# Router of a sparse feed-forward layer: logits of two token tiles in each strip of 32 rows, and one transpose for the logits and for the mask

## The chip, the cores and the metric

The kernel runs on one core of a Trainium2 chip. The time is the device time of one execution in microseconds; the kernel before was measured three times (1661.81, 1661.89 and 1663.59 us, median 1661.89). The engines are named as in the profile: PE is TensorE, PEld its weight loads, DVE VectorE, ACT ScalarE, POOL GpSimd, SP the queue that issues most DMA transfers.

## The reference

All is in float32, for 8 sequences of 512 tokens with 256 channels. Four layers follow one another, each as `x = x + layer(layernorm(x))`: an attention with 16 heads in which only the 307 queries of the highest score spread per head keep a result; an expert layer; a gated linear attention over the sequences as time steps, followed by a gated feed-forward; and the same expert layer once more. The change is in the expert layer:

```python
prob = softmax(xf @ router_w.T + router_b)            # 4096 tokens x 16 blocks
_, idx = top_k(prob, 4)
mask = zeros((n, 16), bool).at[arange(n)[:, None], idx].set(True)
h = einsum('nd,ibd->nib', xf, w1b) + b1b              # 16 blocks of 64 hidden units
h = relu(where(mask[:, :, None], h, 0))
y = einsum('nib,dib->nd', h, w2b) + b2
```

So for each token a router gives 16 logits, the four most probable blocks are kept, and the 64 hidden units of every other block are set to zero. The kernel computes all 1024 hidden units and multiplies them with the mask.

## The kernel before

The residual `xres` stays in SBUF: 128 tokens as partitions, then sequence b (8 of them), slice k (the token's place in its sequence divided by 128, 4 of them) and 256 channels. The attention comes first and takes up to about 585 us; what follows works on one slice k at a time, which is 8 tiles of 128 tokens, one of each sequence, in two groups g of four tiles.

Work on a slice comes as two kinds of Python generators. The "units" are the heavy matmuls: `out_projection` (L780), `routed_ffn` (the hidden layer h_ps at L911, then `down` with y_ps at L891), and `swiglu` (L938). The "pieces" prepare a later slice: `route` (the router) and `gla` (the gated linear attention). `between(units, pieces, n)` issues a unit and then as many pieces, up to the next `yield`, as spread n of them evenly over the units. This sets the program's order roughly; the build then moves neighbouring instructions of an engine by its own costs. Each engine runs its instructions in order. There are eight routers: `route(k, (1, k))` for the first expert layer, `route(k, (2, k))` for the second; ten pieces each.

A router goes like this. The slice's tokens are normalized by ACT (L742), and `to_channels` turns them by PE transposes (L752) into xT[g]: 128 channels as partitions, two halves c, 512 tokens (four tiles of 128). Four matmuls (L810) take the weights `rw[:, c, :]` (128 channels x 32, of which 16 columns are the router's and 16 are zero) as the stationary side and 512 tokens as the moving side; each writes its own strip of 32 PSUM partitions, so the two halves c of a group are in two strips and are not yet summed. ACT copies the 128x512 result to `lgT` (L814). Four matmuls (L820) then turn it: `lgT` in blocks of 128 tokens is the stationary side, and `sel`, 128x32 with ones where two strips' rows belong to one logit, is the moving side; this sums the halves and gives tokens as partitions, with 32 columns (two tiles' 16 logits) for each block. DVE and ACT then compute the softmax (L826 to L839), the top four of each tile (L844, L848: chosen places become 4.0) and the 0/1 mask (L853, 128 tokens x 8 tiles x 16 blocks). Eight PE transposes (L859) turn the mask of each tile into 16 rows of 128 tokens, ACT casts it to bytes (L860, one cast for each group), and two transfers (L864) store it to DRAM as `md[g, j, f, token]`, where block 2f + j covers half j of hidden chunk f. Four transfers (L869) load it back, each row block spread over 64 partitions, as `mk`. In the expert layer ACT (or DVE) makes h from h_ps (L919, L917), and DVE multiplies it with `mk` (L920); then y_ps uses it.

All DMA transfers here are issued by SP, in order. The `post` pool has two buffers for each tag (`lgT` and `mT` have one). At the start of this part SP issues the loads of the weights one after another: rb, rw (L602), w1, b1, w2, b2, q_w and so on; POOL clears `rw` and makes `sel` (L634 to L638); DVE finishes the attention (L628) and uses part of q_w (L681).

## Time and profile before

| what | value |
|---|---|
| median of three runs | 1661.89 us |
| the profiled execution | 1659.83 us |
| its span, first to last instruction | 1658.1 us |
| granted TensorE clock | 0.991 |
| PE busy, of the span | 1605.9 us, 97% |
| DVE busy | 968.2 us, 58% |
| ACT busy | 680.1 us, 41% |
| POOL busy | 334.8 us, 20% |

The profile is of one execution. The busy time of PE counts every pass of a matmul from its start to its modelled end, so passes overlap in it. "The chain that ended last" is found by going back from the last instruction, at each step to what released it or to the instruction before it on its engine; its shares say which engine set the end. In a timeline or a chain a piece is given with its start in us from the span's start, its length and its work. A weight load row (PEld) belongs to the matmul pass behind it. A form such as "128*32 128x512" names the part of the array (rows*columns) and the moving tile.

### The profile page before, as it was taken

The numbers are of one execution on the slowest core, as the hardware profiler recorded it, in microseconds if no ns is written. First come the engines' busy times: TensorE is split into PE (matmuls) and PEld (weight loads), VectorE is DVE, ScalarE is ACT, GpSimd is POOL, SyncE is SP. The second block draws the span as 40 slices with busy tenths as digits, with TensorE's granted clock in tenths as the row PEclk, the third lists the DMA queues.
The fourth block names the chain that finished last, engine by engine and source line by source line (L and its number), as shares of the span: only waits on it lengthen the run. The fifth ranks groups of instructions, "written<-read, shape, count | busy, mean of one in ns | idle before, by whom it ended". The sixth has DMA issues, their size and how long they took to land.

```text
span 1658.1 us, 19533 instructions
## 1 busy us (share of the span) xinstructions
PE 1605.9 (97%) x7298; PEld 823.9 (50%) x7298; DVE 968.2 (58%) x2007; ACT 680.1 (41%) x1216; POOL 334.8 (20%) x384
## 2 busy tenths in 40 slices
PE   7999999999999969999989999999999999999999
PEld 3423323333233247655564556555655655766666
DVE  6977777676666785437663566267265533344242
ACT  2366666666656814352346123622521452121110
POOL 3011111010100112114342342144233320000000
PEclk9999999999999979999999999999999999999999
DMA  3100000000000051010000001000000010011100
GB/s 108 40 2 3 3 2 3 2 3 2 2 3 3 2 164 26 6 34 13 1 1 0 1 1 27 0 0 0 1 1 1 0 26 0 20 33 37 41 26 26
DMA packets 23234, 27.55 MB, mean 17 GB/s; under 512 B 4932, under 2 KB 19684, under 8 KB 23140
## 3 DMA queue, kind: packets, MB, share of 16 engines
q1 hardware_dynamic: 22068, 24.74, 5.1%
q10 hardware_dynamic: 1072, 1.57, 0.3%
q8 instruction: 57, 0.93, 0.2%
q14 instruction: 37, 0.30, 0.1%
HBM read 21.19 MB, written 4.33 MB: 15 GB/s over the span
## 4 chain that ended last, share of the span: by engine, by line
PE 77%; DVE 14%; ACT 3%; POOL 3%; issue 2%; DMA 1%; SPq 0%; ACTq 0%; POOLq 0%; DVEq 0%
PE y_ps L891 16%; PE h_ps L911 11%; PE s L433 8%; PE s L422 8%; PE swi_ps L938 7%; PE proj_ps L1021 7%; PE av L442 7%; DVE pr L1054 2%; DVE pr L1044 2%; PE ao_ps L780 2%; DVE mx L425 2%; PE gla_y L1146 2%; PE q_ps L316 2%; PE v_ps L376 2%; PE k_ps L316 2%
## 5 line engine op out<-in xcount | busy, mean ns | idle before, releaser
L425 DVE TENSOR_REDUCE mx<-s 128x1 f32<-128x512 f32 x512 | 329.0, 684 | 129.0 <-PE s L433 83.0
L437 ACT ACTIVATE e<-s 128x512 f32<-128x512 f32 x512 | 276.1, 599 | 179.1 <-PE s L433 103.5
L422 PE MATMUL s<-k,q 32*128 32x512 f32 x1024 | 298.9, 638 | 2.5 <-ACT k L367 1.8
L433 PE MATMUL s<-q,k 32*128 32x512 f32 x1024 | 294.3, 638 | 0.4 <-DVE mx L425 0.3
L891 PE MATMUL y_ps<-w,h 128*128 128x256 f32 x1024 | 232.2, 382 | 3.5 <-DVE h L920 3.5
L911 PE MATMUL h_ps<-xnT,w 128*128 128x512 f32 x512 | 230.3, 598 | 4.1 <-ACT h L919 4.1
L891 PEld LDWEIGHTS y_ps<-w,h 128*128 128x128 f32 x1024 | 194.1, 192 | 40.9 <-issue 11.1
L911 PEld LDWEIGHTS h_ps<-xnT,w 128*128 128x128 f32 x512 | 95.5, 191 | 114.8 <-issue 106.1
L920 DVE TENSOR_TENSOR h<-h,mk 128x512 f32<-128x512 f32 x128 | 97.8, 777 | 82.2 <-ACT h L919 58.3
L442 PE MATMUL av<-e,va 128*32 128x512 f32 (+1 forms) x1120 | 141.9, 568 | 3.8 <-ACT e L437 2.4
L919 ACT ACTIVATE h<-h_ps,b 128x512 f32<-128x512 f32 x96 | 65.5, 684 | 176.9 <-PE h_ps L911 176.8
L422 PEld LDWEIGHTS s<-k,q 32*128 32x128 f32 x1024 | 89.6, 183 | 84.9 <-DVE mx L425 56.5
L896 DVE TENSOR_TENSOR xres<-xres,y_ps 128x512 f32<-128x512 f32 x48 | 32.8, 684 | 163.6 <-PE y_ps L891 149.3
L433 PEld LDWEIGHTS s<-q,k 32*128 32x128 f32 x1024 | 88.1, 183 | 80.8 <-ACT e L437 53.8
L938 PE MATMUL swi_ps<-zT,w_gate 128*128 128x512 f32 x256 | 122.0, 596 | 4.7 <-DVE h L947 4.6
L938 PE MATMUL swi_ps<-zT,w_up 128*128 128x512 f32 x256 | 121.2, 594 | 0.0
L891 PE MATMUL y_ps<-w_down,h 128*128 128x256 f32 x512 | 116.6, 380 | 0.0
L1021 PE MATMUL proj_ps<-q_w,rT 128*128 128x512 f32 x256 | 116.5, 594 | 0.0
L891 PEld LDWEIGHTS y_ps<-w_down,h 128*128 128x128 f32 x512 | 95.8, 190 | 21.1 <-issue 9.5
L944 ACT ACTIVATE h<-swi_ps 128x512 f32<-128x512 f32 x64 | 38.2, 596 | 157.4 <-PE swi_ps L938 157.3
L1071 POOL TENSOR_TENSOR o<-o,pr 128x512 f32<-128x512 f32 (+2 forms) x56 | 81.1, 1449 | 58.9 <-DVE pr L1054 56.9
L802 POOL TENSOR_TENSOR xres<-xres,b 128x512 f32<-128x512 f32 x32 | 40.0, 1268 | 245.5 <-ACT row L742 223.1
(193 smaller groups left out, 1734.6 us busy)
## 6 DMA issues: line engine op xcount, KB each, us to landing
mk<-md SPq DMA_DIRECT2D x32, 256.0 KB
xres<-in_L_attn_a_x SPq DMA_DIRECT2D x8, 512.0 KB
out<-xres SPq DMA_DIRECT2D x16, 256.0 KB
q<-negT SPq DMA_DIRECT2D x128, 2.0 KB
neg<-negT SPq DMA_DIRECT2D x128, 2.0 KB
w<-in_f_w1T SPq DMA_DIRECT2D x1, 1024.0 KB
w<-in_f_w2T SPq DMA_DIRECT2D x1, 1024.0 KB
w_gate<-in_b_w_gateT SPq DMA_DIRECT2D x1, 1024.0 KB
```

Of the source, the lines that this page charges most:

```text
L316: nc.tensor.matmul(ps, w[:, c, bass.ts(m, P)], xnT[:, c, :], start=(c == 0), stop=(c == NC2 - 1),)
L422: nc.tensor.matmul(s, qs[e][rows, m, bass.ts(k, P)], ks[e][rows, m, :], start=True, stop=True)
L425: nc.vector.tensor_reduce(mx[:, b, 2 * e + m, r : r + 1], s, AX.X, ALU.max)
L433: nc.tensor.matmul(s, ks[e][rows, m, bass.ts(kt, P)], qs[e][rows, m, :], start=True, stop=True)
L437: nc.scalar.activation(ex, s, AF.Exp, scale=1.0 / DH**0.5)
L442: nc.tensor.matmul(av[32 * j : 32 * j + 32, queries], va[:, 8 * kt + 4 * m + j, e, :], es[j][:, queries], start=(kt == 0), stop=(kt == 3 a ...
L891: nc.tensor.matmul(y[0][:, bass.ts(i, D)], h[f][:, bass.ts(2 * u + i, P)], w[:, f, :], start=(f == 0), stop=(f == NF - 1),)
L911: nc.tensor.matmul(ps, w1[:, c, bass.ts(f, P)], xT[g][:, c, :], start=(c == 0), stop=(c == NC2 - 1),)
L920: nc.vector.tensor_tensor(hf, hf, mk[g][:, f, :], ALU.mult)
L938: nc.tensor.matmul(ps, w[:, c, bass.ts(f, P)], zT[g][:, c, :], start=(c == 0), stop=(c == NC2 - 1),)
L1021: nc.tensor.matmul(ps, rT[b // G4][:, c, bass.ts(b % G4, P)], q_w[:, c, m], start=(c == 0), stop=(c == NC2 - 1),)
L1071: nc.gpsimd.tensor_tensor(dst, dst, src, ALU.add)
```

## The change

The logits are summed over the channel halves in PSUM. `rw` gets two versions h of the weights, one with the 16 router columns at places 0 to 15 and one at 16 to 31, zeros elsewhere; the weights are loaded by two transfers. Sixteen matmuls of 128 tokens each go through the four versions (h, c) and, for each, through four tiles: tile b = 2s + h goes to strip s, where all four versions are accumulated into the same 32 rows. So the strips hold the logits of two tiles each, 128x128 in all. `lgT` is 128x128, and one transpose turns it; `sel` is no longer there. The mask is written by two DVE instructions, one for each group, into a tile `taken` whose free axis has the order of `md` (g, j, f, tile). One transpose turns it to 128 rows of 128 tokens, one cast makes bytes of it, and one transfer stores it.

```diff
-        rw = wpool.tile([P, NC2, 32], F32, name="rw")
+        rw = wpool.tile([P, NC2, 2, 32], F32, name="rw")
         nc.gpsimd.memset(rw, 0.0)
-        nc.sync.dma_start(
-            out=rw[:, :, 0:NBLK], in_=t["f_router_wT"].rearrange("(c p) e -> p c e", p=P)
-        )
+        for h in range(2):
+            nc.sync.dma_start(
+                out=rw[:, :, h, bass.ts(h, NBLK)],
+                in_=t["f_router_wT"].rearrange("(c p) e -> p c e", p=P),
+            )
...
-    sel = wpool.tile([P, 2 * NBLK], F32, name="sel")
-    nc.gpsimd.memset(sel, 0.0)
-    for g in range(2):
-        rows = bass.ts(g, 64)
-        nc.gpsimd.tensor_copy(sel[rows, bass.ts(g, NBLK)], i32[rows, 0:NBLK])
...
-        ps = bank_l("lg_ps")
-        for c in range(NC2):
-            for g in range(2):
-                r = 32 * (2 * g + c)
+        ps = bank_l("lg_ps")[:, 0:P]
+        for n in range(2 * NC2):
+            h, c = divmod(n, NC2)
+            for b in range(h, NB, 2):
                 nc.tensor.matmul(
-                    ps[r : r + 32, :], rw[:, c, :], xT[g][:, c, :], start=True, stop=True
-                )
-        lgT = post.tile([P, 512], F32, tag="lgT", name="lgT", bufs=1)
+                    ps[bass.ts(b // 2, 32), :], rw[:, c, h, :],
+                    xT[b // G4][:, c, bass.ts(b % G4, P)],
+                    start=(n == 0), stop=(n == 2 * NC2 - 1),
+                )
+        lgT = post.tile([P, P], F32, tag="lgT", name="lgT", bufs=1)
         nc.scalar.copy(lgT, ps)
         yield
-        ps = bank_l("lg_ps2")[:, 0 : NB * NBLK]
-        for i in range(G4):
-            nc.tensor.matmul(
-                ps[:, bass.ts(i, 2 * NBLK)], lgT[:, bass.ts(i, P)], sel, start=True, stop=True
-            )
+        ps = bank_l("lg_ps2")[:, 0:P]
+        nc.tensor.transpose(ps, lgT, ident)
...
-        nc.vector.tensor_scalar(pr, prob[:, :, 0:NBLK], 2.0, None, ALU.is_ge)
+        taken = post.tile([P, 2, 2, NF, G4], F32, tag="pr", name="taken")
+        for g in range(2):
+            nc.vector.tensor_scalar(
+                taken[:, g],
+                prob[:, bass.ts(g, G4), 0:NBLK].rearrange("p i (f j) -> p j f i", j=2),
+                2.0, None, ALU.is_ge,
+            )
         yield
-        mT = post.tile([NBLK, 2, 512], U8, tag="mT", name="mT", bufs=1)
-        for g in range(2):
-            ps = bank_l("mT_ps")
-            for i in range(G4):
-                nc.tensor.transpose(ps[0:NBLK, bass.ts(i, P)], pr[:, 2 * i + g, :], ident)
-            nc.scalar.copy(mT[:, g, :], ps[0:NBLK, :])
+        ps = bank_l("mT_ps")[:, 0:P]
+        nc.tensor.transpose(ps, taken.rearrange("p g j f i -> p (g j f i)"), ident)
+        mT = post.tile([P, P], U8, tag="mT", name="mT", bufs=1)
+        nc.scalar.copy(mT, ps)
...
-        for j in range(2):
-            nc.sync.dma_start(out=md[:, j].rearrange("g f l -> f g l"), in_=mT[j::2])
+        nc.sync.dma_start(out=md.rearrange("g j f (i t) -> (g j f i) t", t=P), in_=mT)
```

## The prediction

> **What bounds the kernel now.** I read the page first (share of each engine, then the chain that ended last), then that chain cut to single stages, then the rows of the tiles that the change touches.

> ```profile
> span 1658.1 us, 19533 instructions
> PE 1605.9 (97%) x7298; PEld 823.9 (50%) x7298; DVE 968.2 (58%) x2007; ACT 680.1 (41%) x1216; POOL 334.8 (20%) x384
> PE 77%; DVE 14%; ACT 3%; POOL 3%; issue 2%; DMA 1%; SPq 0%; ACTq 0%; POOLq 0%; DVEq 0%
> ```

> TensorE (PE) is busy for 97% of the span and carries 77% of the chain. A busy PE need not be a useful one, so I ask what it does at the router. Here is the chain between 1420 and 1545 us, where the routers of slices 2 and 3 run beside an expert layer; the columns are start, duration and work, and "x8" counts passes.

> ```profile
> 1423.47 0.87 PE mT_ps L859 x8
> ...
> 1441.97 0.44 PE chT_ps L752 x4
> ...
> 1453.64 6.87 PE h_ps L911 x16
> 1460.51 0.99 PE lg_ps L810 x8
> 1461.51 5.35 PE h_ps L911 x12
> 1466.86 0.81 PE lg_ps L820 x8
> 1467.67 1.80 PE h_ps L911 x4
> 1469.46 13.81 PE y_ps L891 x64
> 1483.28 0.87 PE mT_ps L859 x8
> ```

> There is nothing but PE in this stretch: each piece begins where the last one ended, so a microsecond of router work is a microsecond of the kernel. The stage sums say where else that holds (length, then busy us and instructions of PE, PEld, DVE, ACT, POOL):

> ```profile
> 605.00:760.00 155.00, 154.93 (x627) 103.21 (x628) 76.54 (x268) 62.57 (x107) 23.80 (x28) 0.99 0.12 38
> 980.00:1060.00 80.00, 78.97 (x333) 51.61 (x333) 38.53 (x112) 37.95 (x65) 21.25 (x23) 1.00 0.06 14
> 1320.00:1658.00 338.00, 334.15 (x1244) 216.83 (x1242) 121.21 (x300) 74.37 (x123) 19.95 (x16) 1.00 0.09 26
> ```

> All eight routers lie in these three stages. The stages between them, where DVE, ACT and POOL lead the chain, hold none; they start from a PE result and so begin earlier by what PE gained before.

> **The change part by part.** The rows of the tiles (duration min/median/max in ns):

> ```profile
> L810 PEld LDWEIGHTS lg_ps<-xnT,rw x64: 106/108/109, 629.6 to 1520.3; 128*32 128x32 f32 x64
> L810 PE MATMUL lg_ps<-xnT,rw x64: 592/605/617, 629.6 to 1520.7; 128*32 128x512 f32 x64
> L820 PE MATMUL lg_ps<-sel,lgT x64: 192/276/276, 632.4 to 1527.2; 128*128 128x32 f32 x64
> L859 PE MATMUL mT_ps<-ident,pr x64: 272/272/273, 641.1 to 1543.7; 128*16 128x128 f32 x64
> L860 ACT CAST mT<-mT_ps x16: 557/570/575, 641.7 to 1544.1; 16x512 uint8<-16x512 f32 x16
> ```

> There are 64 passes in 8 routers at each line, so 8 a router: an f32 matmul is two passes (4 matmuls at L810 and at L820), a transpose is one (8 at L859; L752's "0.44 x4" is 0.109 us for each transpose).

> *Turning the logits (L820).* Four matmuls, 8 passes: 0.81 us in the chain, and the four h_ps passes behind them take 1.80 instead of 4 x 0.429 = 1.72, since their weights still queue. Together 0.89. One 128x128 transpose, at L752's 0.109, replaces them: 0.78 saved.

> *Turning the mask (L859).* Eight transposes, 0.87, become one, 0.11: 0.76 saved.

> *The logits (L810).* Four matmuls over 512 columns become sixteen over 128, i.e. 8 passes become 32. Each of the four strips of 32 output rows gets 8 passes of 128 columns where it had 2 of 512; the columns streamed are the same. Now 0.99 us in the chain (from the first pass's start to the last one's last column 0.90: two times 0.429 and a stagger of some 7 ns a strip; the rest is the array emptying), and 0.20 more behind it (12 h_ps passes take 5.35, not 5.15). A pass of 128 columns costs 0.109 in L859's and L752's rows, so 8 x 0.109 and the same stagger make 0.89: no change, if the weights of the next pass load under the running one and the strips stay side by side. The trace has no strip pass of 128 columns. The nearest row is gh_ps (L985), same form, two strips with four passes each:

> ```profile
> 725.44 0.14 PEld L985 LDWEIGHTS gh_ps<-rT,q_wg 128*32 128x32 f32 x4 [0.33 <-issue]
> 725.90 0.12 PEld L985 LDWEIGHTS gh_ps<-rT,q_wg 128*32 128x32 f32 x2 [0.31 <-issue]
> 726.33 0.12 PEld L985 LDWEIGHTS gh_ps<-rT,q_wg 128*32 128x32 f32 x2 [0.31 <-issue]
> 725.44 1.91 PE L985 MATMUL gh_ps<-rT,q_wg 128*32 128x512 f32 x8
> ```

> Loads start 0.43 apart, that is one pass apart, and all 8 passes take 1.91 with their draining, 4 x 0.43 and 0.2: the loads lie under the passes, though both use the same rows of the array. [...]

> *Per router* 0.78 + 0.76 + 0 = 1.54; times 8, **12.3 us**.

> *ACT.* The copy lgT shrinks from 128x512 to 128x128, and two casts of 16x512 (0.57 each, 1.05 together) become one of 128x128; ACT's own 128x128 row (L832, 0.31) prices the cast. ACT idles before both and PE comes to L820 two or more units later, so neither counts, but in two places. Slice 2 of the first round: at 723.67 PE waits 0.35 for an ACT row that stands behind the casts; mT to that row shortens by about 0.92 against PE's own 0.76: 0.16 more. Slice 3 of the first round is the next point.

> *The mask's store and load (L864, L869).* Two stores with 0.74 us between their issues become one, of 128 rows of 128 bytes instead of 32 of 512. At 1002 us this is on the chain (cast, SP, store 1.79, load 4.13, then the multiplies L920, then a PE wait of 1.03 at 1015.0). From the first mT pass to the second mask load's issue is 4.26 us now; 0.27 + 0.04 + 0.31 for transpose and cast, 1.8 + 0.2 for a store with 8 small packets an engine (30 ns each now), 0.6 for the first load's issue make 3.3: some 1 us earlier. With L820's 0.78 the mask comes 1.7 earlier where PE comes 1.54 earlier, so that wait stays and 0.1 more is gained. If small packets cost 1 us, it is a loss of 0.9. SP has one entry less a router, nothing else moves past it but the last output of a slice, which stands behind the store now.

> *DVE.* One threshold (L853, 0.23) becomes two of 64 columns, at about 0.2 each: 0.2 more. In the first round L853 ends 0.24, 0.60 and 0.17 us before PE starts mT in slices 0, 2 and 3, elsewhere 0.95 or more, and both sides start from L820, so PE may wait 0.1 or so in one or two routers, inside the 0.1 above and the range. The multiplies L920 behind it have eight buffers.

> *The split router.* For slice 0 of the second round the build's order puts one y_ps matmul inside the sixteen. The chain now shows 1.94 there, as the fourth matmul waits for xnT; the 0.43 of y_ps fills that wait, less a second emptying of the array (0.1 each way and a weight load): 0.2 gained.

> *Start.* rw comes by two transfers ahead of w1, 256 more packets of 64 bytes: about 0.6 us later for all loads behind it. The first user is L681 at 598.40, whose weights land at 597.55, so 0.85 hides it; past that each 0.1 costs 0.1. The two sel copies and a memset on POOL cover nothing. DVE's order there puts the last outC product ahead of one 0.2 us product: 0.2 gained.

> Sum: 12.3 + 0.16 + 0.1 + 0.2 + 0.2 = 13.0. The profiled execution took 1659.83 (span 1658.1 and 1.7 around it), so 1646.8; the median of the runs stands 2.06 above it: **1648.9 us**, 0.8% faster. A difference under 0.2%, 3.3 us, is no change here.

> **The rivals.**
> [...]
> *Gain given back off PE:* if the four routers of the first round yield nothing since DVE and POOL lead later (760 to 980, 1060 to 1320), half is left: about 1655. Against it: those stretches start from PE results.
> *Slower:* strips lose their overlap at 32 short passes, because PE can't start loads and passes quickly enough. [...] Against it, at L810 eight loads begin within 0.05 us.
> *The change is not felt:* PE's order is as described in the built program; only mask latency (1 us at 642, 721, 1002 each) could eat some 3 us: 1652.

> **How the numbers follow.** Forecast, with small errors and the mask's latency, 0.73 (1645.5 to 1652.5); weights not hidden 0.08; given back 0.07; slower 0.09; no change from causes I don't see 0.03. Faster 0.87 (a hair off the first three), same 0.04, slower 0.09. The range 1645.5 to 1656 holds the first three cases but for their tails, about 0.8.

> **What would show it.** L820's and L859's successors with 8 passes each over the run, 0.11 in the chain; the logits at 1.0 in the chain with 256 passes over the run, and h_ps behind them as now; loads of one strip 0.11 apart. The stretch from the end of one y_ps group to the next (1409.65 to 1469.46 now, 59.8 us) shorter by 1.5. Wrong if the logits' piece is near 1.8 or 3.6, if PE waits for L920's successor at 654 or 1015 for longer, or if DVE waits for the weights at 598.

## The result, and the profile after

| | median us | range | runs |
|---|---|---|---|
| before | 1661.81 | 1660.41 to 1663.59 | 5 |
| after | 1651.50 | 1648.13 to 1653.55 | 5 |

The ratio is 0.9936, with a 95% interval from 0.9922 to 0.9950: 10.3 us less, 0.64%. The forecast was 1648.9, so it comes out 2.6 us above it and inside the range. Against the forecast's gain of 13.0 us, 2.7 are missing; the interval allows gains from 8.3 to 13.0.

The profiled execution of the changed kernel was the longest of its five, 1653.55 us (span 1651.8). The profiled execution of before, 1659.83 us, was on the other side, 2.0 us under the median of before. So profile against profile only 6.3 us are to be seen, and these two must not be read as the result. First the engines' totals and shares of the chain, on the page after:

```profile
span 1651.8 us, 19680 instructions
PE 1599.0 (97%) x7378; PEld 820.1 (50%) x7378; DVE 969.4 (59%) x2015; ACT 671.7 (41%) x1208; POOL 334.3 (20%) x381
PE 77%; DVE 14%; ACT 3%; POOL 3%; issue 1%; DMA 1%; SPq 0%; ACTq 0%; POOLq 0%; DVEq 0%
```

The bound is the same, PE at 97% of the span. Now the chain that ended last, after, in the stretch of the routers of slices 2 and 3 in the second round (start, duration, work):

```profile
1407.11 13.81 PE y_ps L889 x64
1420.92 0.11 PE mT_ps L857
1421.03 12.02 PE h_ps L909 x28
...
1450.34 6.87 PE h_ps L909 x16
1457.20 1.01 PE lg_ps L806 x32
1458.21 5.35 PE h_ps L909 x12
1463.56 0.11 PE lg_ps L816
1463.67 1.72 PE h_ps L909 x4
1465.39 13.81 PE y_ps L889 x64
1479.20 0.11 PE mT_ps L857
```

Each turned matrix is one pass of 0.11 us instead of eight passes of 0.87 and 0.81. The four h_ps passes behind the logits' transpose take 1.72, no longer 1.80. The logits, 32 passes now, take 1.01 where 8 long ones took 0.99. From one y_ps group to the next it is 1465.39 - 1407.11 = 58.28 us; it was 59.81. That is 1.53 less, and the forecast was 1.54. The rows of the tiles, after (minimum, median and maximum in ns):

```profile
L806 PEld LDWEIGHTS lg_ps<-xnT,rw x256: 106/110/110, 631.6 to 1516.1; 128*32 128x32 f32 x128
L806 PE MATMUL lg_ps<-xnT,rw x256: 272/273/297, 631.6 to 1516.2; 128*32 128x128 f32 x128
L816 PE MATMUL lg_ps<-ident,lgT x8: 272/272/328, 634.4 to 1521.7; 128*128 128x128 f32 x8
...
L859 ACT CAST mT<-mT_ps x8: 261/265/265, 642.6 to 1537.7; 128x128 uint8<-128x128 f32 x8
L862 SPq DMA_DIRECT2D md<-mT x8: 326/336/347, 642.9 to 1538.0; - x8
```

There are 256 passes at L806 and one transpose a router, as the program says. ACT's cast is 0.265 (forecast 0.31).

To see where the 2.7 us went, I lined up the same PE instruction in both traces. The table gives the change of each stage's length (the starts named are those of before; the first stage starts with the span). The third column is the trace of a kernel that comes up below, the changed one with a single matmul more.

| stage | forecast | after | with one unread matmul |
|---|---|---|---|
| 0 to 638.5 | -0.98 | +1.18 | +0.56 |
| 638.5 to 753.1 | -4.00 | -2.72 | -2.73 |
| 753.1 to 876.3 | 0 | +0.39 | +0.41 |
| 876.3 to 1086.4 | -1.64 | -2.01 | -2.06 |
| 1086.4 to 1306.7 | 0 | +3.33 | +0.02 |
| 1306.7 to 1639.7 | -6.36 | -6.54 | -6.54 |
| sum | -12.98 | -6.37 | -10.34 |

Two stages stand out. The second misses 1.3 us: it holds the mask of slice 0 and the routers of slices 1 and 2 in the first round, and the miss lies in slice 2 (below). The fifth holds no router at all and lost 3.3. The first stage differs between executions by far more than the change can make (four traces of the changed kernel or of it with an idle time filled begin the instruction at 638.5 by +1.18, -0.62, +3.20 and +0.56 against before's). Half clock has a part in it: ahead of 638.5 these four show 23.9, 23.9, 34.1 and 30.7 us of it, before's trace 17.1. It is not all, since the first two have the same and differ by 1.8; how much of this scatter is left in a median stays open.

The fifth stage is a matter of the granted clock. In the view of windows (length, then busy us and instructions of PE, PEld, DVE, ACT and POOL, then the granted clock, DMA share and GB/s), before:

```profile
1155.00:1170.00 15.00, 12.93 (x56) 8.92 (x55) 10.52 (x21) 7.65 (x12) 5.64 (x4) 1.00 0.00 1
1185.00:1215.00 30.00, 30.00 (x110) 17.41 (x109) 4.39 (x13) 12.82 (x23) 2.34 (x4) 1.00 0.00 1
```

and after:

```profile
1155.00:1170.00 15.00, 12.93 (x55) 10.06 (x55) 9.23 (x20) 5.89 (x8) 3.91 (x4) 0.89 0.00 0
1185.00:1215.00 30.00, 30.00 (x102) 16.94 (x102) 3.63 (x12) 11.30 (x20) 2.34 (x4) 0.94 0.00 1
```

A mean of 0.89 over 15 us is about one step of 3.4 us at half clock (the granted clock of after is 0.50 from 1157.74 to 1161.15), and 0.94 over 30 us is the same once more (0.50 from 1195.28 to 1198.70). At each of them the shift of the instructions behind grows (by 1.63 us at 1158 and 1.69 at 1195), and it is not made good by the end. All thirteen traces of changed kernels agree: those with both steps have +3.3 in this stage, those with one +1.3 to +1.7, and those with none between -0.02 and +0.04.

### The profile page after: what moved, and what is told of

Read it like the earlier page. It is cut to its first block, busy times and chain, and to the rows that moved or that the text cites. A ratio compares the mean times of both kernels' runs of the same rounds, so it can differ in the third digit from the quotient of the medians.

```text
span 1651.8 us, 19680 instructions
## 1 busy us (share of the span) xinstructions
PE 1599.0 (97%) x7378; PEld 820.1 (50%) x7378; DVE 969.4 (59%) x2015; ACT 671.7 (41%) x1208; POOL 334.3 (20%) x381
## 4 chain that ended last, share of the span: by engine, by line
PE 77%; DVE 14%; ACT 3%; POOL 3%; issue 1%; DMA 1%; SPq 0%; ACTq 0%; POOLq 0%; DVEq 0%
PE y_ps L889 16%; PE h_ps L909 11%; PE s L433 8%; PE s L422 8%; PE swi_ps L936 7%; PE proj_ps L1019 7%; PE av L442 7%; DVE pr L1052 2%; DVE pr L1042 2%; PE ao_ps L775 2%; PE q_ps L316 2%; PE gla_y L1144 2%; DVE mx L425 2%; PE v_ps L376 2%; PE k_ps L316 2%; POOL o L1069 1%
## 5 line engine op out<-in xcount | busy, mean ns | idle before, releaser
L918 DVE TENSOR_TENSOR h<-h,mk 128x512 f32<-128x512 f32 x128 | 97.6, 774 | 78.9 <-ACT h L917 70.0
```

The source lines that it names most:

```text
L918: nc.vector.tensor_tensor(hf, hf, mk[g][:, f, :], ALU.mult)
```

## The experiments

The times of before beside the experiments: 1661.47 for the first four, 1661.88 for the next four, 1662.12 and 1660.82 for the last two pairs. Differences are to the changed kernel's median where nothing else is said.

### One part alone

The mask part alone: the logits by the four long matmuls and `sel` as before, the mask by one transpose, one cast, one store.

```diff
-        ps = bank_l("lg_ps")[:, 0:P]
-        for n in range(2 * NC2):
...
+        ps = bank_l("lg_ps")
+        for c in range(NC2):
+            for g in range(2):
...
-        nc.tensor.transpose(ps, lgT, ident)
+        for i in range(G4):
+            nc.tensor.matmul(
+                ps[:, bass.ts(i, 2 * NBLK)], lgT[:, bass.ts(i, P)], sel, start=True, stop=True
+            )
```

> The kernel before with the mask's part of the change alone (thresholds in the stored order, one transpose, one cast, one store); the logits as before. My theory (PE passes removed are time removed): 0.76 us less of PE a router, 6.1 us in all, so about 1655.7 against 1661.8; in the chain mT is 0.11 instead of 0.87, and at the first router of slice 3 the wait of PE for the masked h falls from 1.03 to below 0.5. Rival (the gain comes from the shorter store and casts, not from PE): the gain would sit at slice 3 of the first round alone, some 1 to 2 us in all, 1660. Since DVE's order in slice 2 of the first round is the one of the changed kernel here, I expect the wait of the logits for xnT there too, about 0.5 us or more lost.

The logits part alone: the mask by eight transposes, two casts and two stores as before.

```diff
-        nc.tensor.transpose(ps, taken.rearrange("p g j f i -> p (g j f i)"), ident)
-        mT = post.tile([P, P], U8, tag="mT", name="mT", bufs=1)
-        nc.scalar.copy(mT, ps)
+        mT = post.tile([NBLK, 2, 512], U8, tag="mT", name="mT", bufs=1)
+        for g in range(2):
+            ps = bank_l("mT_ps")
+            for i in range(G4):
+                nc.tensor.transpose(ps[0:NBLK, bass.ts(i, P)], pr[:, 2 * i + g, :], ident)
+            nc.scalar.copy(mT[:, g, :], ps[0:NBLK, :])
```

> The changed kernel with the mask's part as before; the logits in two tiles a strip and one transpose for them. My theory: 0.78 us less of PE a router, 6.2 us in all, about 1655.6; the sixteen short matmuls cost the 1.0 us of the four long ones. Additive with the mask's part to the 10.3 us of the whole within the noise of 1 to 2 us. DVE's order in slice 2 of the first round is that of the kernel before, so no wait of the logits for xnT there. Rival (sixteen short matmuls cost more than four long ones): less than 5 us of gain.

The two halves number the tiles differently, so in both of these kernels the mask goes to other tiles of tokens than it should; the work is the same. Measured: 1655.90 for the mask alone (ratio 0.9968, 0.9956 to 0.9979), 5.6 us less than before; 1654.99 for the logits alone (0.9965, 0.9951 to 0.9978), 6.5 less. Both parts are worth about what their passes are worth (6.1 and 6.2 were expected), and the sum, 12.1, is near the forecast's 12.3 + 0.7. The whole change gives some 2 us less than its parts one by one; each part's interval is about 2 us to either side, so this difference is not clear of noise. Neither part's trace has the half-clock stretches at 1158 and 1195.

The rows of PE's waits also separate the parts. With the mask alone, then with the logits alone (in all, times, longest, in us):

```profile
PE y_ps L895 <- DVE h L924: 2.8, 3, 1.9
```

```profile
PE y_ps L885 <- DVE h L914: 3.6, 3, 1.9
```

The difference is one wait, that for slice 3's mask at 1013: it is 0.35 us with one transpose, cast and store, and 1.13 with the logits alone. Before and after, in timelines (start, duration, work, and in brackets the idle time ahead of it):

```profile
1015.00 3.72 PE L891 MATMUL y_ps<-w,h 128*128 128x256 f32 x16 [1.03 <-DVE h L920]
```

```profile
1011.74 3.63 PE L889 MATMUL y_ps<-w,h 128*128 128x256 f32 x14 [0.46 <-DVE h L918]
```

The shorter mask path takes this wait down by more than half, where the forecast let it stay.

### The disputed pass cost: all logits passes twice

```diff
-        for n in range(2 * NC2):
+        for n in [*range(2 * NC2)] * 2:
```

> The changed kernel with the sixteen logits matmuls of each router done twice over (the second pass of them starts the sum anew, so the result is the same). It prices them by itself. My theory (four strips side by side, weights loaded under the running pass): 8 passes of 0.109 a strip, 0.87 us a router more, 7.0 us in all: 1658.5 against the 1651.5 of the changed kernel. If weight loads of a strip stood between its passes: 1.73 a router, 13.8 in all, 1665. If the strips went one after another: 3.5 a router, 28 in all, 1680.

The stop and start marks are repeated too, so the second round writes the same sums over the first. The chain of this kernel:

```profile
1456.47 1.88 PE lg_ps L806 x64
...
1515.63 1.89 PE lg_ps L806 x64
```

The 32 extra passes cost 1.88 - 1.01 = 0.87 us a router, 8 steps of 0.109 for four strips: they run side by side, and their weight loads of 0.110 lie under them. The total is 1654.72 (0.9962, 0.9949 to 0.9974), only 3.2 more than the changed kernel instead of 7.0. From 1306.7 on, where four routers lie, its trace is 3.50 us longer than the changed kernel's, four times 0.87. In the total the four others seem to cost next to nothing; part of that is that this trace again has no half-clock stretch at 1158 and 1195 (3.3 us in the changed kernel's), the rest was not followed up.

### Are the strips side by side because of the order?

```diff
-        for n in range(2 * NC2):
-            h, c = divmod(n, NC2)
-            for b in range(h, NB, 2):
+        for s in range(4):
+            for n in range(2 * NC2):
+                h, c = divmod(n, NC2)
+                b = 2 * s + h
```

> The changed kernel with the loops of the logits turned round: the strip is the outer loop, so the eight passes of one strip of 32 rows stand behind one another in PE's program, and the passes of the next strip behind them; the same 32 passes, loads and sums. Theory A (PE works on the four strips at once only where passes of different strips stand next to each other in its program): 32 passes one behind another at 0.109 us, so 3.5 us a router in the chain instead of 1.01, 2.5 x 8 = 20 us more: about 1671.5. Theory B (a strip's passes may overlap the next strip's whatever the order): at most 1.0 in the chain, 1651.5 as the changed kernel. In between, where PE looks a few passes ahead: each strip's last pass overlaps the next strip's first, 29 passes' time, 3.2 us, 1669.

```profile
1459.53 2.39 PE lg_ps L807 x32
```

1658.55 us (0.9981, 0.9975 to 0.9988), 7.0 more than the changed kernel, and 1.38 us more a router in the chain. (Eight times 1.38 is 11.0; this trace too is without the stretches at 1158 and 1195.) It lies between the two theories: not 3.5, and not 1.0. The starts of the passes of one router, in us from the first, read from the traces:

```
changed kernel: 0.000 0.006 0.013 0.020   0.133 0.140 0.146 0.153   0.242 0.249 0.255 0.262 ... 0.808
strip outside:  0.000 0.134 0.243 0.352   0.461 0.467 0.570 0.600   0.679 0.709 0.789 0.819 ... 2.189
```

Four passes alone, then pairs: with the strip outside, about the last four passes of a strip run beside the first four of the next. By this pattern PE worked here on two strips with four passes of one between them in the program, not on all four. The overlap of the strips is bought by the order of the change's loops, and here it is worth 1.38 us a router. Which pass belongs to which strip is not in the records; the four is read from the pattern.

### DVE's order in slice 2

Before, four small DVE products for the gated linear attention of the first slice stood ahead of both xnT copies of that router. In the changed kernel the build put them (L968 to L971) between the two copies. One of them took long, and the logits waited for the second copy. The chain of after:

```profile
704.46 0.59 DVE rr L968
705.08 1.76 DVE rr L969
706.86 0.21 DVE rr L970
707.10 0.17 DVE rr L971
707.26 0.61 DVE xnT L751
707.92 1.07 PE lg_ps L806 x28
```

Before, this product of 128x8 took 0.21 us. POOL was adding a bias to the residual beside it:

```profile
705.52 1.27 POOL L797 TENSOR_TENSOR xres<-xres,b 128x512 f32<-128x512 f32 x1
```

In all eleven traces in which DVE's order is this one, the product takes 1.73 to 1.75 us and ends 0.02 to 0.03 us behind this POOL instruction. With the logits alone, where DVE's order is that of before, it takes 0.21. That fits a product that must wait for POOL; no run took POOL's instruction away to test it.

PE's timelines of this router, before and after, show where its gain went:

```profile
708.35 1.06 PE L810 MATMUL lg_ps<-xnT,rw 128*32 128x512 f32 x8
709.34 1.98 PE L911 MATMUL h_ps<-xnT,w 128*128 128x512 f32 x4
711.16 0.97 PE L820 MATMUL lg_ps<-sel,lgT 128*128 128x32 f32 x8
...
719.79 1.04 PE L859 MATMUL mT_ps<-ident,pr 128*16 128x128 f32 x8
720.67 1.30 PE L752 MATMUL chT_ps<-ident,row 128*128 128x128 f32 x10
```

```profile
707.23 0.41 PE L806 MATMUL lg_ps<-xnT,rw 128*32 128x128 f32 x4
707.92 1.07 PE L806 MATMUL lg_ps<-xnT,rw 128*32 128x128 f32 x28 [0.27 <-DVE xnT L751]
708.91 1.98 PE L909 MATMUL h_ps<-xnT,w 128*128 128x512 f32 x4
710.89 0.33 PE L816 MATMUL lg_ps<-ident,lgT 128*128 128x128 f32 x1
...
719.06 0.30 PE L857 MATMUL mT_ps<-ident,taken 128*128 128x128 f32 x1
719.20 1.25 PE L747 MATMUL chT_ps<-ident,row 128*128 128x128 f32 x10
```

The logits, torn in two, take 1.68 where they took 0.99, and the step to their transpose, which now waits for ACT's copy, 1.98 where it was 1.82: 0.85 us lost. From the logits' transpose to the mask's it is 8.17 where it was 8.63. PE alone would have come 0.28 earlier, but the mask from DVE was not there. The mask's single pass then gave its 0.74 in full, and the stretch behind it 0.07. In all 0.42.

The experiment makes the products wait for the copy:

```diff
         rr = small("rr")
+        if k == 0:
+            nc.scalar.copy(rr[0:1, 0:1], ready[1, 2][0][1][0:1, 0, 0:1])
         nc.scalar.activation(rr, mv[:, :, 1], AF.Sqrt)
```

> The changed kernel, and an ACT copy of one element that makes DVE's small products of the first attention slice (L968 to L971) stand behind the second xnT copy of the router of slice 2, first round, instead of ahead of it; one 1-element copy on ACT is added. Theory (slice 2's router gave only 0.42 us of the forecast 1.70 because its logits waited for xnT behind those products): the logits' piece is in one again, PE's wait of 0.27 at 708 is gone, and the start of L997 at about 728 comes 1.1 to 1.3 us sooner against the start of the y_ps group ahead of it; in the total 1650.3, which the spread of the runs may hide. Rival (that router lost its gain elsewhere, in the wait for the rows behind the transposes): the start of L997 moves by less than 0.3 and the total stays at 1651.5.

1652.59 us (0.9941, 0.9928 to 0.9954): nothing gained. The wait of the logits is gone, and they take 1.02 again, but this row is new among PE's waits:

```profile
PE mT_ps L857 <- DVE taken L850: 1.6, 1, 1.6
```

From the instruction at 638.5 to L997 at 728 this kernel is 2.12 us shorter than before, the changed one 2.72: 0.6 lost, where 1.1 to 1.3 was expected. So moving the product is no remedy. What sets mT in this slice is the softmax and top-four chain of DVE and ACT, which runs between multiplies L918: before, its last product ended 0.60 us ahead of the mask's first transpose; in the changed kernel, and here, PE starts 0.15 after it. Of this slack PE can gain 0.45 at most as long as the chain takes as long. And here it took longer: from the logits' transpose to the end of the mask 9.03 us against 8.02, with DVE waiting 1.42 for ACT's exponential (L826), which stood behind four rows L737 that need the moved products. So this run does not say what the router would give with the copy in time and all else the same. The logits alone, with DVE's order of before, lost nothing in the stage from 638.5 to 753.1 (1.53 of 1.56 us); the mask alone, with the new order, got 0.40 of 2.44.

### The half-clock stretches

The first thought was the long idle time of PE ahead of ao_ps, 3.0 us at 606; three matmuls that nothing reads were put there:

```diff
+            warm = acc("warm")
+            for _ in range(3):
+                nc.tensor.matmul(
+                    warm, ident, outC[5][:, 0, :], start=True, stop=True
+                )
```

> The changed kernel with three matmuls added, whose result nothing reads, on PE between the attention's last product and the output projection, where PE stands idle for 3.0 us. Nothing else of the order changes. Theory of the clock (part of what the forecast missed is half-clock stretches of PE that begin in its idle times, here 604.8 to 611.6 in the profile of the changed kernel): PE is busy just before 606, the half-clock stretch is missing or ends sooner, and the output projection from 606 on runs at 0.43 us for each matmul's two passes from the start; 1.7 to 2.7 us less, 1649 to 1650. Rival (the 128x256 matmuls are slow there because of transfers of the weights, not the clock): nothing gained, 1651.5, or up to 0.5 us lost.

1651.76 (0.9946, 0.9933 to 0.9958), no gain. The half clock at the start lasted from 584.7 to 608.6 in its trace and from 584.3 to 611.6, with a break of 6.8, after; the stretches at 772, 841, 1158 and 1196 were there.

Then I put all stretches of all traces together. After 600 us each starts at a whole number of steps of 3.413 us from the others of its trace, and each lasts one or two such steps (in after at 772.03, 840.30, 1157.74 and 1195.28, the last three 20, 113 and 124 steps behind the first; the granted clock is 0.50 there for 3.41, 6.82, 3.41 and 3.42 us). From the PE rows I worked out which share of each step PE was busy, in all 14 traces of this case, from 615 us on (some 4180 steps at full clock). Of 25 steps that were busy for less than 0.42, all 25 were followed by a step at half clock. Of 5 between 0.42 and 0.46, two were. Of the rest five were, all of them fully busy steps (four at about 1190, one at 728). These five have one thing in common: most of the step is al_ps, of the form 32*128, that is on 32 of the array's 128 rows. In the changed kernel's step from 1191.87 to 1195.28 PE runs:

```profile
1191.47 1.99 PE L997 MATMUL al_ps<-q_wg,gh 32*128 32x256 f32 x12
1193.39 0.70 PE L889 MATMUL y_ps<-w_down,h 128*128 128x256 f32 x2
1194.02 1.13 PE L997 MATMUL al_ps<-q_wg,gh 32*128 32x256 f32 x4
```

An estimate from the same rows puts all 32 cases in one order: let a pass count for the time its columns take (0.429 us for 512, as 16 passes of h_ps take 6.87) times the share of the array that it uses by its form. Then the 28 lowest steps, up to 0.363, were all followed by half clock, 4 of the 13 from 0.365 to 0.417 were, and none of the 4145 above. The five fully busy steps thus stand among the idle ones. That the share of the array counts beside idle time is a reading of this order, made from the traces afterwards; no run was made to test it. Whether one idle time of 2.07 us, 0.61 of a step, leaves a step busy for less than 0.42 hangs on where the grid falls (in five of eleven traces it did, see below). By the trace of after, one of the idle times behind 1100 costs 1.63 us.

The idle time is the one ahead of the transposes L1136. Before, it ran from 1158.33 to 1160.40 and a step began at 1158.51: 1.89 us in one step, busy 0.445, no half clock. After, it ran from 1155.19 to 1157.26 inside the step from 1154.32 to 1157.74, busy 0.39. The row behind it, before and after:

```profile
1160.40 0.63 PE L1138 MATMUL oT_ps<-ident,o 128*128 128x128 f32 x4 [2.07 <-DVE o L1129]
```

```profile
1157.26 0.66 PE L1136 MATMUL oT_ps<-ident,o 128*128 128x128 f32 x4 [2.07 <-DVE o L1127]
```

The idle time is 2.07 us in eleven of the fourteen traces, before's among them. In five it lay whole in one step, and all five have the half clock behind it; in six the grid cut it, 1.89 us at most in one step, and none has. The place of the grid against the program's start differs from trace to trace, by anything from 0.0 to 2.9 us of a step's 3.4, so where it falls looks like chance. That is as true of the kernel before, of which there is one trace.

A first try to fill idle times was aimed badly:

```diff
+    def keep_busy(x, n):
+        ps = bank_l("unread")[:, 0:D]
+        for _ in range(n):
+            nc.tensor.matmul(ps, x[:, 0:P], w2[:, 0, :], start=True, stop=True)
...
+                if w is w2 and not last and (k, g, u, i, f) == (2, 0, 0, 0, 6):
+                    keep_busy(h[5], 4)
...
+            if not last and (k, g, f) == (3, 1, 7):
+                keep_busy(h[5], 8)
```

> The changed kernel with 12 matmuls (24 passes, 256 columns each) that nothing reads, in two places where PE stands idle: four ahead of the y_ps matmul that waits 1.94 us for DVE at 770, eight ahead of the h_ps matmul that waits 4.09 us for ACT at 837.4. Otherwise PE's order is the same. In the traces so far, each stretch of half clock begins on a grid of 3.413 us, one grid step after a step in which PE was busy for less than some 0.43 of the time (772.0 after 0.45 busy, 840.3 after 0.15), and steps with more than 0.5 are followed by none. Theory (idle PE brings the half clock): with the idle time filled no stretch of half clock begins near 772 or 840; the first gives back 1.7 us (3.41 at half clock), the second 2.8 (5.65 us of PE's work at half clock), together 4.5: about 1647. Rival (the half clock comes from something else, or the work behind it waits for DVE anyhow): the stretches stay, or go and the total stays: 1651.5.

By the trace the matmuls stood one slice later than meant, at 813 and at 1066, so the text above names places that this kernel did not fill. It still told something. Its PE waits:

```profile
PE oT_ps L1145 <- DVE o L1136: 5.2, 3, 2.1
...
PE h_ps L918 <- ACT h L926: 2.5, 1, 2.5
```

The 1.7 us at 813 made the wait for ACT 2.5 instead of 4.1, at no cost, and no half-clock step followed at 840; but then the transposes at 845 waited 1.93 us for DVE, and PE came to 849 at the same time (-3.44 us against before; -3.32 in a second trace of the changed kernel, with the half clock at 840). That half clock is covered by DVE. The eight matmuls at 1066, where PE has no idle time, cost their whole 3.4 us. In all 1652.72 (0.9942, 0.9930 to 0.9954).

Beside it ran the changed kernel, unaltered:

> The changed kernel once more, unaltered, for the spread of its times and a second trace. Theory (the place of the 3.413 us grid against the program differs between executions, so stretches of half clock come and go): median 1651.5 within 1 us, with single times between 1648 and 1654; the second trace has another set of such stretches, and it and the first differ in length by about half the difference of the summed half-clock time. Rival (the stretches belong to the kernel): the same stretches at 772, 840, 1158 and 1195, and times within 0.1%.

1651.75 us, from 1648.27 to 1652.64 (0.9933, 0.9921 to 0.9945). Its trace has the stretches at 770, 838, 1155 and 1193 again: against the theory, the set hardly differs from the first, only the start does. So they are not the first execution's alone.

Then a single matmul ahead of the idle time at 1157. PE runs it at 1149, and what stands behind it moves that much into the idle time:

```diff
+            if w is w_gate and (k, g, f) == (1, 1, 2):
+                nc.tensor.matmul(
+                    bank_l("unread")[:, 0:256], zT[g][:, 0, 0:P], w_down[:, 0:1, :],
+                    start=True, stop=True,
+                )
```

> The changed kernel with one matmul more (two passes of 256 columns, 0.43 us) that nothing reads, put where PE stands idle for 2.07 us ahead of the transposes L1136 at 1157; the order of every engine is otherwise the same. In the traces a step of the 3.413 us grid with PE busy 0.45 or less is followed by a step at half clock; with 0.46 or more there was none behind this idle time. The idle time is now 1.64 us, so a step that holds all of it is busy at least (3.41 - 1.64) / 3.41 = 0.52. Theory (the gain missing from the changed kernel went in part to a half-clock step behind this idle time, 1.63 us, and to one 11 steps later, 1.7 us, which was seen only where the first was): no half-clock step near 1158 or 1195 in the trace; no loss from the added matmul; median 1.6 to 3.3 us under the changed kernel run beside it, about 1649. Rival (such a step costs the end nothing, or comes whatever PE does): a step at 1158 all the same, or the median equal to the changed kernel's.

> The changed kernel unaltered, beside the kernel with one matmul more in its idle time, for a median on the same chip. Theory: 1651.6, with a half-clock step behind the idle time at 1157 where that lies within one step of the grid. Rival: as the kernel beside it.

With the matmul 1648.73 us (1647.97 to 1650.32; ratio to before 0.9918, 0.9904 to 0.9931); without, on the same chip, 1650.77 (1649.65 to 1651.49; 0.9928, 0.9916 to 0.9941). That is 2.0 us in the medians and 1.65 in the means of five and five, with a 95% interval of about 0.4 to 2.9. The windows of the kernel with the matmul:

```profile
1155.00:1170.00 15.00, 13.41 (x59) 9.96 (x60) 10.77 (x27) 5.12 (x8) 5.07 (x4) 1.00 0.00 0
1185.00:1215.00 30.00, 30.00 (x107) 18.01 (x107) 4.46 (x14) 10.67 (x18) 2.34 (x4) 1.00 0.00 1
```

PE's idle time is 1.74 now (1.64 was expected), the step is busy 0.49, and both stretches are gone; the stage that had +3.33 has +0.02. The idle time lay whole in one step here too, and no half clock came. In its third trace, taken here, the unaltered kernel had neither stretch: the grid cut the idle time (0.58 busy). So the stretch at 1158 comes with some executions of the changed kernel (two of three traces), not with all, and the one trace taken beside the filled kernel does not show it: that the difference of the medians is this step is argued, though its size fits. The kernel before with the same matmul was not run.

### More idle times filled

The same remedy for the idle time at 770 (1.94 us), two matmuls more in the right place, and then four more at 813:

```diff
+                if w is w2 and not last and (k, g, u, i, f) == (1, 1, 0, 0, 6):
+                    keep_busy(h[5], 2)
+                if w is w2 and not last and (k, g, u, i, f) == (2, 0, 0, 0, 6):
+                    keep_busy(h[5], 4)
```

> The changed kernel with the unread matmul at 1157 (0.43 us) and two more (four passes, 0.86 us) ahead of the y_ps matmul that waits 1.94 us for DVE at 770, this time in that very place; the order of every engine is otherwise the same. The two idle times at 770 (1.94 and 0.50, 0.70 apart) then leave a step of the grid that holds both busy at least (3.41 - 1.58) / 3.41 = 0.54. Theory: no half-clock step near 772 and none near 1158. Where the trace with the step at 772 is compared with the one without, PE reached the stage of 876 some 1.7 to 2.1 us earlier without it, so 1.7 us less than the kernel with one unread matmul (1648.7) in those executions in which the step comes, about 1 us in the median: 1647.5. Rival (the stage of 770 to 880 is set by POOL and DVE, and what PE gains there it waits): 1648.7.

> As the kernel with three unread matmuls, and four more (eight passes, 1.72 us) in the y_ps group at 813, where an earlier run had them: PE then waits 1.7 us less at 837 and no half-clock step followed at 840. Theory: no half-clock step near 772, 840 and 1158; the first oT_ps transposes at 848 wait about 1.9 us for DVE instead, as in that run, and so the median is at most 0.4 us under that of the kernel with three: 1647.1. Rival: the eight passes cost their 1.72 us, 1649.2.

The first has the line for 770 alone, the second both; both have the matmul at 1157. 1648.09 us (1647.47 to 1649.20; 0.9922, 0.9909 to 0.9936) and 1647.68 (four runs, 1646.34 to 1647.87; 0.9916, 0.9903 to 0.9930). In both traces the step behind 770 is at full clock. The window there after, and in the kernel with all seven:

```profile
765.00:780.00 15.00, 12.56 (x49) 9.90 (x48) 14.12 (x20) 0.69 (x1) 11.03 (x11) 0.89 0.12 35
```

```profile
765.00:780.00 15.00, 13.42 (x61) 10.98 (x60) 14.12 (x20) 0.69 (x1) 11.04 (x11) 1.00 0.13 35
```

PE's stage from 753.1 to 876.3 is 1.95 us shorter than before in both traces, where the changed kernel's was 0.39 longer (its third trace, without the step at 772, has -1.67). The last kernel is 13.1 us under before (1660.82 beside it), where the changed one was 10.1 to 11.4 under it: 1.8 to 3.0 better. They did not run side by side, and the intervals of their ratios overlap. The steps between the three filled kernels, 0.6 and 0.4, are too small to be told apart by these runs. The first of the two has a half-clock step at 1190 without one at 1153, so the claim in an expectation above, that the second stretch comes only with the first, is wrong; this step too stands behind the al_ps passes of the estimate above.

## Why the prediction came out as it did

- *Turning the logits, turning the mask (0.78 and 0.76 a router):* right. 1.53 in the chain where 1.54 was forecast, and the four routers of the second round, from 1306.7 on, gave 6.54 where 6.36 was booked. The parts alone measured 5.6 and 6.5 us.
- *The logits, sixteen short for four long at no cost:* right. 1.01 against 0.99, and 0.87 for each 32 passes more. Loads of 0.110 us stand 0.109 apart under the passes of their own strip, also where one strip's passes follow one another. No run shows the term behind "weights not hidden", the range's end at 1656 and the sign "near 1.8", a load of 0.11 between the passes of a strip, nor the 3.6 of 32 passes without overlap: the runs show 1.01 in their place, and 2.39 with the loops turned round. There the strips do lose part of their overlap, as the rival "slower" has it, for 1.38 us a router, where 32 passes of 0.109 in a row would have added 2.5.
- *DVE ("PE may wait 0.1 or so in one or two routers, inside the 0.1 above"):* this is the step that failed. Two waits in slice 2 were mis-sized. The logits' wait for DVE's second xnT copy stood at nothing, since DVE was taken to keep its order; the build moved a product that then took 1.76 us ahead of that copy, and 0.85 was lost. The wait for the mask, for which the text gave the slack of 0.60 and allowed 0.1, took 0.28. With 0.15 of small shortfalls, 0.42 of 1.70 came: 1.3 us lost.
- *ACT, 0.16 in slice 2:* part of that router, and 0.07 of it came.
- *The mask's store and load (0.1):* mis-sized to the good side. The wait for slice 3's mask fell from 1.03 to 0.46 instead of staying; the stage gained 2.0 where 1.64 was forecast.
- *The split router and the start (0.2 each):* the second round gained 6.54 against 6.36. The 0.2 at the start can't be told: that stage differs by more from one execution to the next.
- *What the sum lacked:* the clock. Nothing in it said that the idle time of 2.07 us at 1157, where it falls whole into one step of the 3.413 us grid, would be followed by a step at 0.50 of the clock, which cost 1.63 us in the trace of after. This explains most of why the profiles show 6.3 and not 10.3. It does not explain the medians: before has the same idle time of 2.07, and nothing shows that its other executions escape the step.
- *So of the 2.7 missing* the stages account for 0.7: 1.3 lost in slice 2, less 0.4 at the mask's wait and 0.2 in the second round. The other 2.0 are within the interval; whether they are clock, at the start or at 1158 and 1195, stays open. That the result lies in the range owes something to the range's width of 7 us, though the parts of the sum that were priced by passes came out to within 0.1 us a router.
- *"Gain given back off PE"* expected half of the first round's gain to be lost between the routers. It was not: the stage from 1086.4 to 1306.7 shows 0.0 in the traces without half-clock steps there, and the one from 753.1 to 876.3 +0.4, 0.0 and -1.7 in the changed kernel's three traces, the last without the step at 772.

## What to carry to other kernels

A small matmul that only turns or sums something should be counted in passes: here eight passes made one were worth seven times 0.11 us where PE set the time (0.87 to 0.11 for the mask), and 32 short passes to four strips cost no more than 8 long ones (1.01 and 0.99) with neighbours in the program on different strips, but 2.39 with one strip's passes in a row. A gain ahead of a wait is capped by the slack of the engine that is waited for: where the profile shows 0.6 us of it, book no more than that up to this wait. Ask too whether the build will order that engine's work as before; here one product put ahead of a copy cost 0.85. And where PE idles for about 2 us in an otherwise dense stretch, look at the granted clock behind it: here one matmul of 0.43 us that nothing reads went into the idle time at 1157, and the median was 2.0 us lower, though that the step at half clock is the cause is argued, not shown.
